# Four-layer graph network on one core: another order of the gate products in layer 0, another start and end of layer 3

## The chip, the cores and the metric

The kernel runs on one core of one Trainium2 chip, in one launch. The metric is device time in microseconds (us), the median of three runs; lower is better. A core has five engines that run side by side and are synchronised by semaphores: TensorE (matrix products and transposes, written PE in the profile; PEld is its loading of weights), VectorE (DVE), ScalarE (ACT), GpSimd (POOL) and SyncE (SP, which only issues transfers here). Matrix products land in PSUM banks[...]; everything else lives in the 128 partitions of SBUF.

## What is computed

The input x has 128 x 64 = 8192 tokens of 256 channels, all float32: 128 graphs of 64 nodes. Four layers of graph networks are applied in turn, each as

```
x = x + layer(relu(layernorm(x)))
```

Layer 0 is two graph convolutions, and then four LSTMs with windows of p = 1, 2, 3, 4 nodes, each of which writes the last state of every window back into the nodes:

```python
h = relu(einsum('ts,bsh->bth', adj, x @ Wg0 + bg0))
h = relu(einsum('ts,bsh->bth', adj, h @ Wg1 + bg1))
for p in range(1, 5):
    nw = Tv // p
    wins = h[:, :nw * p, :].reshape(Bv * nw, p, Hd)
    last = lstm_last(Wih[p-1], Whh[p-1], bih[p-1], bhh[p-1], wins)
    h = h.at[:, arange(nw) * p + (p - 1), :].set(last.reshape(Bv, nw, Hd))
# one step of the LSTM
g = x_t @ Wih.T + h @ Whh.T + bias          # gates i, f, gg, o of 256 channels each
c = sigmoid(f) * c + sigmoid(i) * tanh(gg)
h = sigmoid(o) * tanh(c)
```

Layer 1 is an attention over 512 edges with 4 heads. Layer 2 is a graph convolution, a product with W1, a batch norm with ReLU, a product with W2 and a second batch norm (over all tokens). Layer 3 is an attention over the 64 nodes of each graph:

```python
Wh = einsum('bnf,fo->bno', h, W)
e = leaky_relu((Wh @ a1)[:, :, None] + (Wh @ a2)[:, None, :], 0.2)
e = where(adj == 0, -inf, e)
out = einsum('bij,bjo->bio', softmax(e), Wh)
```

## The kernel before

The tokens are worked on in 16 chunks of 512 (`NCH`), or, in the LSTMs, in 4 groups of 2048 (`NGR`). A framework's scheduler puts the instructions of each engine into an order and sets the semaphores; an instruction that is wrapped in `late(...)` keeps its place in the order in which the program names it. So the order on an engine is in part written out and in part the scheduler's. Each engine then runs its own list strictly in order.

**The LSTMs of layer 0** take from 193 to 1281 us. The product of a gate (256 input channels by 256 output channels, both halved) is made with seven block products instead of eight, of inputs that are sums and differences of the halves (`xop` for the inputs, `lstm_h` for the state, computed in `prepare` and `gate_done`). The weights are combined in the same way by GpSimd and VectorE when a new window begins (line L434). A `Step` is one time step t of a window length w for one part of the tokens; its gates are i, gg, f, o, or only i, gg, o at t = 0, where there is no earlier state. A matmul of a product has 512 columns for w = 1, 256 for w = 2 and 4, and 336 for w = 3. For t = 0 a product is one matmul (with the input), for t > 0 two (input, state), all issued by L643. The trace shows each matmul as two passes.

The two halves of the groups are done one after the other, and in each half w = 1, 2, 3, 4. Within a window length the steps alternate between two parts of the tokens: t = 0 of one part, t = 0 of the other, t = 1 of the one, and so on. Such a pair of parts is what is called a pair below; w = 1 and 2 have two pairs per half, w = 3 and 4 one. There are 184 gates, 48 of them with t = 0 and w > 1.

`gate` is a generator that makes a gate's seven products, in four portions, with three accumulators in PSUM: `pa` (3 banks in turn), `pb` (2 banks) and `pc` (3 banks). The result goes to four blocks of the tile `gate`:

- products 1 (to `pa`) and 2 (to `pb`); then the copy of `pa` on ScalarE (L686), the addition of `pb` on VectorE (L687) and the gate's function, sigmoid or tanh, on ScalarE (L671)
- product 6, on top of 1 in `pa`; the copy of that sum on ScalarE (L691); product 7 to `pc` and the copy of it on ScalarE (L693)
- product 5, on top in `pa`; VectorE adds the sum to the copy of `pc` (L696)
- product 3, on top in `pa`, and the function straight from the bank (L671); product 4 on top in `pc`, VectorE adds it to the copy of L691 (L701), and the function of the two second blocks (L671). Then `gate_done` does the elementwise work of the cell.

Each of these products writes to a bank that the copy before it reads, so product 6 waits for L686, product 5 for L691, product 3 for L696, and product 4 for L693. A new gate waits until a bank of `pa` has been read by the last L671 of an older gate.

The slots of the loop (L805 and on) interleave three gates: in every slot a new one begins, the one before it (the middle) does its third portion, and the oldest ends:

```python
one = step.gate(new[1]); next(one)        # new gate: products 1, 2
if len(flight) > 1:
    next(flight[-1][1])                   # middle gate: product 5
    old = flight.pop(0)
    next(old[1], None)                    # oldest gate: products 3, 4
...
next(one)                                 # new gate: products 6, 7
```

`prepare` of the next step (copies by ScalarE, L624, differences by VectorE, L626 and after) is called near the end of the step before.

**The end of layer 2** leaves its output, before the last batch norm, in the first of the two tiles of each chunk's `hs`, and the batch norm as a scale and a shift per channel (`scale2`, `shift2`), which are known only when the last chunk's sums are in.

**Layer 3** takes from 1931 us to the end. For a chunk n, `fetch` loads the residual x; `second_norm` scales layer 2's output to the tile `o` (pool `xin2`, 4 buffers; chunk 0 on VectorE, L1598, and ScalarE, L1601, all others on GpSimd, L1606), transposes it into two banks (`pair`, L1613), adds the residual (L1615), takes mean and variance of each tile of 128 tokens (L1619, L1620), takes the inverse root by power on GpSimd (L1622 to L1626) and normalises (L1630 on GpSimd; chunk 0 L1634 on ScalarE). `features` transposes the result back (L1645) with ReLU on ScalarE (L1648); `project3` makes Wh, with one column more for the node's own score (two matmuls of 257 columns per tile, in halves of two tiles); `dense_scores` makes the scores and their exponentials; `turn` transposes these; `dense_values` makes the weighted sums (L50 into `pair`), divides and adds the residual (L1719) and stores 512 KB (L1727). The main loop runs the chunks in a pipeline: `second_norm(n + 2)`, `features(n + 1)`, `project3(n)`, `turn(n - 1)`, the rest of `project3(n)`, `dense_scores(n)`, `dense_values(n - 1)`, for n from -2 on. Transfers are issued on SyncE, but for the intermediate x of layer 0, which GpSimd issues.

Of the kernel before, what the change touches and what calls it, by code (L numbers as in the profile page):

```python
# [30 lines left out]
def gnn_stack_kernel(ctx: ExitStack, tc: tile.TileContext, a: dict, out: bass.AP):  # L31
# [25 lines left out]
    def token_tiles(ap, n=0):  # L57
        return ap[n * CHUNK : (n + 1) * CHUNK, :].rearrange("(i p) d -> p i d", p=P)
# [12 lines left out]
    def late(ins):  # L71

        tc.keep_in_program_order(ins)
# [334 lines left out]
    with ExitStack() as l0:  # L408
# [178 lines left out]
        class Step:  # L587
# [90 lines left out]
            def gate(self, q):  # L678
# [14 lines left out]
                nc.scalar.copy(blk[1, 1], pc[:, :N])  # L693
# [115 lines left out]
        for slot in range(len(tasks) + 2):  # L809
# [5 lines left out]
            if len(flight) > 1:  # L815
                next(flight[-1][1])
                old = flight.pop(0)
                next(old[1], None)
            elif flight and not new:
                old = flight.pop(0)  # L820
                next(old[1], None)
            else:
                old = None
                if flight:
                    next(flight[-1][1])
# [475 lines left out]
    with ExitStack() as l2:  # L1301
# [282 lines left out]
        def as_tokens(t):  # L1584
            return t.rearrange("p c t -> p (c t)").rearrange("p (i d) -> p i d", i=4)
# [4 lines left out]

        def second_norm(n):


            xt, v = xts[n], hs[n][0]
            half = (0, 1) if n % 2 == 0 else (1, 0)
            o = xin2.tile([P, 2, CHUNK], F32, tag="xin2", name="o")
            if n == 0:
                nc.vector.tensor_scalar(  # L1598
                    o[:, 0, :], v[:, half[0], :], scale2[:, 0:1], shift2[:, 0:1], ALU.mult, ALU.add
                )  # L1600
                nc.scalar.activation(  # L1601
                    o[:, 1, :], v[:, half[1], :], AF.Identity, bias=shift2[:, 1:2], scale=scale2[:, 1:2]
                )
            else:
                for c in range(2):
                    nc.gpsimd.tensor_scalar(  # L1606
                        o[:, c, :], v[:, half[c], :], scale2[:, c : c + 1], shift2[:, c : c + 1], ALU.mult, ALU.add
                    )
            p = pair_bank()
            for i in range(4):  # L1610
                for c in range(2):
                    k = (i % 2 * 2 + c) * P
                    nc.tensor.transpose(p[:, i // 2, k : k + P], o[:, c, i * P : (i + 1) * P], ident)  # L1613
            flat = xt.rearrange("p i d -> p (i d)")
            nc.vector.tensor_tensor(flat, p.rearrange("p b d -> p (b d)"), flat, ALU.add)  # L1615
            st = stat.tile([P, 4, 6], F32, tag="ln_st", name="ln_st")
            mv = stat.tile([P, 4, 2], F32, tag="ln_mv", name="ln_mv")
            for i in range(4):
                nc.vector.bn_stats(st[:, i, :], xt[:, i, :])  # L1619
                nc.vector.bn_aggr(mv[:, i, :], st[:, i, :])  # L1620
            rs = stat.tile([P, 4], F32, tag="ln_rs", name="ln_rs")
            nc.gpsimd.tensor_scalar(rs, mv[:, :, 1], 1e-5, None, ALU.add)  # L1622
            nc.gpsimd.tensor_tensor(rs, rs, half_power, ALU.pow)
            nm = stat.tile([P, 4], F32, tag="ln_nm", name="ln_nm")
            nc.gpsimd.tensor_tensor(nm, mv[:, :, 0], rs, ALU.mult)
            nc.gpsimd.tensor_scalar(nm, nm, -1.0, None, ALU.mult)  # L1626
            h = norms[n] = as_tokens(v)
            for i in range(4):
                if n:
                    nc.gpsimd.tensor_scalar(  # L1630
                        h[:, i, :], xt[:, i, :], rs[:, i : i + 1], nm[:, i : i + 1], ALU.mult, ALU.add
                    )
                else:
                    nc.scalar.activation(  # L1634
                        h[:, i, :], xt[:, i, :], AF.Identity, bias=nm[:, i : i + 1], scale=rs[:, i : i + 1]
                    )
# [75 lines left out]
        def dense_values(n):  # L1712
# [14 lines left out]
            nc.sync.dma_start(out=token_tiles(out, n), in_=xt)  # L1727
# [3 lines left out]
        for n in range(-2, NCH + 1):  # L1731
            if 4 <= n + 4 < NCH:
                fetch(n + 4)
            if n + 2 < NCH:
                second_norm(n + 2)
            if 0 <= n + 1 < NCH:
                features(n + 1)
# [77 lines left out]
```

## Time and profile before

| | us |
|---|---|
| median of 3 runs | 2097.78 |
| range of the runs | 2097.69 to 2099.34 |
| the profiled execution, whole | 2098.59 |
| its span in the trace | 2096.8 |

| stretch of the trace | from, to (us) | length | TensorE busy |
|---|---|---|---|
| layer 0, graph convolutions | 0 to 193 | 193.0 | 182.6 |
| layer 0, LSTMs | 193 to 1280.9 | 1087.9 | 1060.0 |
| layer 1 | 1280.9 to 1705 | 424.1 | 408.1 |
| layer 2 | 1705 to 1931 | 226.0 | 220.7 |
| layer 3 | 1931 to 2096.8 | 165.8 | 146.4 |

The span is what lies between the first and the last instruction of the trace, the profiled execution's own time is a little longer, and both stand for one execution among the runs. The mean clock that TensorE was granted is 0.988 of full speed over the span, and 0.93 in layer 3. Names such as `pa`, `pb`, `pc`, `bank` and `pair` in the profile are PSUM buffers, `gate`, `xop`, `lstm_h`, `o` and `h` tiles in SBUF. "L643" is line 643 of the kernel; a row `PE pa L643 <- ACT gate L691` is idle time of TensorE before a matmul of L643 into `pa` that ended with ScalarE's instruction of L691, with the total in us, the number of such waits and the longest.

### The profile page before, as it was taken

The numbers are of one execution on the slowest core, as the hardware profiler recorded it, in microseconds if no ns is written. First come the engines' busy times: TensorE is split into PE (matmuls) and PEld (weight loads), VectorE is DVE, ScalarE is ACT, GpSimd is POOL, SyncE is SP. The second block draws the span as 40 slices with busy tenths as digits, with TensorE's granted clock in tenths as the row PEclk, the third lists the DMA queues.
The fourth block names the chain that finished last, engine by engine and source line by source line (L and its number), as shares of the span: only waits on it lengthen the run. The fifth ranks groups of instructions, "written<-read, shape, count | busy, mean of one in ns | idle before, by whom it ended". The sixth has DMA issues, their size and how long they took to land.

```text
span 2096.8 us, 25494 instructions
## 1 busy us (share of the span) xinstructions
PE 2017.9 (96%) x9444; PEld 1356.4 (65%) x9444; DVE 1348.9 (64%) x2453; ACT 1186.4 (57%) x2264; POOL 321.3 (15%) x432
## 2 busy tenths in 40 slices
PE   8999999999999999999999998999999899999898
PEld 6776488866688746886667885333334775444686
DVE  8764666564655576556546555676766777886675
ACT  4344766554655468566546553666665456591454
POOL 3000010100200020002000002214323520001662
PEclk9999999999999999999999999999999999999899
DMA  9231000100100350001001006113224851022012
GB/s 314 93 96 51 0 21 1 41 0 1 40 1 1 105 177 21 1 1 41 0 0 41 1 1 226 61 51 96 81 76 120 254 191 51 1 80 81 31 61 71
DMA packets 94444, 135.06 MB, mean 64 GB/s; under 512 B 6384, under 2 KB 82032, under 8 KB 92144
## 3 DMA queue, kind: packets, MB, share of 16 engines
q1 hardware_dynamic: 87600, 109.11, 15.8%
q0 software_dynamic: 6112, 24.12, 3.8%
q8 instruction: 74, 1.21, 0.2%
q14 instruction: 50, 0.41, 0.1%
q10 hardware_dynamic: 608, 0.20, 0.0%
HBM read 87.28 MB, written 46.14 MB: 64 GB/s over the span
## 4 chain that ended last, share of the span: by engine, by line
PE 84%; ACT 5%; DVE 5%; issue 4%; DMA 1%; POOL 1%; ACTq 0%; POOLq 0%; DVEq 0%; SPq 0%
PE pa L643 25%; PE bank L50 12%; PE pc L643 12%; PE pb L643 6%; PE bank L947 5%; PE pa L1360 5%; PE pair L963 5%; PE bank L1141 3%; PE bank L979 2%; PE pc L1360 2%; ACT gate L671 2%; PE pair L50 1%; PE pb L1360 1%; ACT gate L723 1%; PE pair L1121 1%
## 5 line engine op out<-in xcount | busy, mean ns | idle before, releaser
L643 PE MATMUL pa<-xop,sih 128*128 128x256 f32 (+2 forms) x1056 | 347.4, 418 | 11.0 <-ACT gate L691 9.4
L671 ACT ACTIVATE gate<-gate,bias 128x256 f32<-128x256 f32 (+2 forms) x368 | 246.9, 678 | 181.2 <-DVE gate L687 97.5
L643 PEld LDWEIGHTS pa<-xop,sih 128*128 128x128 f32 x1056 | 199.3, 191 | 85.1 <-issue 20.9
L643 PE MATMUL pc<-xop,wih 128*128 128x256 f32 (+2 forms) x736 | 251.5, 423 | 0.0
L643 PE MATMUL pa<-lstm_h,shh 128*128 128x256 f32 (+1 forms) x672 | 212.6, 398 | 0.0
L687 DVE TENSOR_TENSOR gate<-pb,gate 128x256 f32<-128x256 f32 (+2 forms) x184 | 87.6, 476 | 162.2 <-PE pb L643 126.3
L970 DVE SCALAR_TENSOR_TENSOR lr<-lr 128x1024 f32<-128x1024 f32 x128 | 150.3, 1217 | 63.9 <-ACT lr L969 57.8
L643 PEld LDWEIGHTS pc<-xop,wih 128*128 128x128 f32 x736 | 140.1, 190 | 51.4 <-issue 22.5
L701 DVE TENSOR_TENSOR gate<-pc,gate 128x256 f32<-128x256 f32 (+2 forms) x184 | 87.7, 477 | 119.8 <-PE pc L643 118.3
L969 ACT COPY lr<-pair 128x1024 f32<-128x1024 f32 x128 | 123.0, 1013 | 49.8 <-PE pair L963 48.9
L643 PEld LDWEIGHTS pa<-lstm_h,shh 128*128 128x128 f32 x672 | 127.7, 190 | 30.2
L643 PE MATMUL pc<-lstm_h,whh 128*128 128x256 f32 (+1 forms) x448 | 141.8, 398 | 0.0
L686 ACT COPY gate<-pa 128x256 f32<-128x256 f32 (+2 forms) x184 | 76.8, 417 | 104.0 <-PE pa L643 103.4
L671 ACT ACTIVATE gate<-pa,bias 128x256 f32<-128x256 f32 (+2 forms) x184 | 94.6, 514 | 72.4 <-PE pa L643 71.4
L963 PE MATMUL pair<-sd_hot,xq 64*128 64x512 f32 x512 | 128.0, 619 | 2.3 <-ACT lr L969 2.3
L947 PE MATMUL bank<-wlv,hT 128*128 128x512 f32 x256 | 118.4, 605 | 0.2 <-ACT hT L156 0.2
L696 DVE TENSOR_TENSOR gate<-pa,gate 128x256 f32<-128x256 f32 (+2 forms) x184 | 87.5, 476 | 35.3 <-PE pa L643 33.1
L643 PE MATMUL pa<-xop,wih 128*128 128x256 f32 (+1 forms) x320 | 101.8, 400 | 5.6 <-ACT xop L624 3.1
L434 POOL TENSOR_TENSOR sih<-wih 128x512 f32<-128x512 f32 x8 | 10.4, 1306 | 630.5 <-DMA wih<-in_WihT 630.5
L643 PE MATMUL pb<-xop,wih 128*128 128x256 f32 (+1 forms) x320 | 100.9, 399 | 0.0
L643 PEld LDWEIGHTS pc<-lstm_h,whh 128*128 128x128 f32 x448 | 85.1, 190 | 20.1
L693 ACT COPY gate<-pc 128x256 f32<-128x256 f32 (+2 forms) x184 | 76.3, 415 | 32.5 <-PE pc L643 31.0
(321 smaller groups left out, 3820.9 us busy)
## 6 DMA issues: line engine op xcount, KB each, us to landing
field<-sd_hot SPq DMA_DIRECT2D x8, 1152.0 KB, 10.7
wih<-in_WihT SPq DMA_DIRECT2D x8, 1024.0 KB, 4.9
xres<-in_x SPq DMA_DIRECT2D x16, 512.0 KB, 5.9
xa<-xres POOLq DMA_DIRECT2D x16, 512.0 KB
xin<-xb SPq DMA_DIRECT2D x16, 512.0 KB, 3.9
h<-xb SPq DMA_DIRECT2D x16, 512.0 KB, 3.9
out_x<-h SPq DMA_DIRECT2D x16, 512.0 KB, 2.9
xin<-in_x SPq DMA_DIRECT2D x15, 512.0 KB, 7.5
```

The costliest lines, as they stand in the source:

```text
L50: nc.tensor.matmul(o, lhsT, rhs, start=start, stop=stop)
L643: ins = nc.tensor.matmul(p[:, : self.N], weights[kind, self.phase](k, q), x[k], start=first_ and kind == "ih", stop=kind == "hh" or not se ...
L671: nc.scalar.activation(out, in_, AF.Tanh if q == 2 else AF.Sigmoid, bias=bias[:, self.w - 1, 2 * q + j : 2 * q + j + 1],)
L686: nc.scalar.copy(blk[0, 0], pa[:, :N])
L687: nc.vector.tensor_tensor(blk[0, 0], pb[:, :N], blk[0, 0], ALU.add)
L696: nc.vector.tensor_tensor(blk[1, 1], pa[:, :N], blk[1, 1], ALU.add)
L701: nc.vector.tensor_tensor(blk[1, 0], pc[:, :N], blk[1, 0], ALU.add)
L947: ins = nc.tensor.matmul(p, hTs[n][:, k, i * P : (i + 1) * P], wlv[:, k, :], start=k == 0, stop=k == 1)
L963: ins = nc.tensor.matmul(p[:, par, :], queries[it][r, c * P : (c + 1) * P], sd_hot[r, :], start=True, stop=True)
L969: nc.scalar.copy(lr, p)
L970: nc.vector.scalar_tensor_tensor(lr, lr, 0.2, lr, ALU.mult, ALU.max)
L1360: ins = nc.tensor.matmul(p, lhs[k], x[k], start=first_, stop=last_one, skip_group_check=True)
```

## The change

It has four parts.

1. In each slot of the LSTM loop, the oldest gate's last portion (products 3, 4) is now asked for before the middle gate's product 5, so that a slot is: new 1, 2; oldest 3, 4; middle 5; new 6, 7.
2. The copy of product 7 from `pc` is done by VectorE for steps with t = 0 and w > 1, by ScalarE otherwise.
3. Layer 3 has a `first_norm` for chunk 0 alone. It works by pairs of tiles (256 tokens): half-width scalings on VectorE and ScalarE, four transposes into one bank, addition, mean and variance, the root by ScalarE's Sqrt and VectorE's reciprocal, the normalisation on ScalarE, and then transposes back and ReLU by pair. The scaling of the other chunks is a function of its own, `scale_o`, still on GpSimd, and is called two chunks ahead of `second_norm`, for chunks 1 to 3 ahead of everything else. Chunk 1 takes its root like chunk 0, and has two of its four tiles normalised by ScalarE and two by GpSimd. For chunks 1 and 2 some instructions keep their place (`late`), and for chunk 0 the first projection (tiles 0, 1) comes before `second_norm(2)`, the second after it.
4. The last chunk's result is stored in two halves, each after its two tiles, instead of in one.

```diff
@@ gate
-                nc.scalar.copy(blk[1, 1], pc[:, :N])
+                (nc.vector.tensor_copy if not self.t and self.w > 1 else nc.scalar.copy)(blk[1, 1], pc[:, :N])
@@ the slot loop
             if len(flight) > 1:
-                next(flight[-1][1])
                 old = flight.pop(0)
                 next(old[1], None)
+                next(flight[-1][1])
@@ layer 3
+        def first_norm():
...
+            for ip in range(2):
+                r = slice(ip * 256, (ip + 1) * 256)
+                late(nc.vector.tensor_scalar(
+                    o[:, 0, r], v[:, 0, r], scale2[:, 0:1], shift2[:, 0:1], ALU.mult, ALU.add
+                ))
+                late(nc.scalar.activation(
+                    o[:, 1, r], v[:, 1, r], AF.Identity, bias=shift2[:, 1:2], scale=scale2[:, 1:2]
+                ))
+            def add(ip):
+                p = bank()
...
+                        ins = nc.tensor.transpose(
+                            p[:, (2 * i + c) * P : (2 * i + c + 1) * P], o[:, c, k : k + P], ident
+                        )
...
+                late(nc.vector.tensor_tensor(flat, p, flat, ALU.add))
+            def sums(ip):
+                i2 = slice(2 * ip, 2 * ip + 2)
+                for i in (2 * ip, 2 * ip + 1):
+                    late(nc.vector.bn_stats(st[:, i, :], xt[:, i, :]))
+                    late(nc.vector.bn_aggr(mv[:, i, :], st[:, i, :]))
+                late(nc.scalar.activation(rs[:, i2], mv[:, i2, 1], AF.Sqrt, bias=eps))
+            def root(ip):
+                i2 = slice(2 * ip, 2 * ip + 2)
+                late(nc.vector.reciprocal(rs[:, i2], rs[:, i2]))
+                late(nc.vector.scalar_tensor_tensor(
+                    nm[:, i2], mv[:, i2, 0], -1.0, rs[:, i2], ALU.mult, ALU.mult
+                ))
+                for i in (2 * ip, 2 * ip + 1):
+                    late(nc.scalar.activation(
+                        h[:, i, :], xt[:, i, :], AF.Identity, bias=nm[:, i : i + 1], scale=rs[:, i : i + 1]
+                    ))
+            add(0)
+            sums(0)
+            add(1)
+            root(0)
+            sums(1)
+            root(1)
+            yield
...
+            for ip in range(2):
+                p = bank()
...
+                late(nc.scalar.activation(
+                    hT[:, :, ip * 256 : (ip + 1) * 256].rearrange("p c (i t) -> p i c t", i=2),
...
+                    AF.Relu,
+                ))
+                yield
+        def scale_o(n):
...
+            for c in range(2 if n else 0):
+                late(nc.gpsimd.tensor_scalar(
+                    o[:, c, :], v[:, half[c], :], scale2[:, c : c + 1], shift2[:, c : c + 1], ALU.mult, ALU.add
+                ))
         def second_norm(n):
...
+            keep = late if n < 3 else lambda ins: ins
...
+            yield
...
+            if n == 1:
+                keep(nc.scalar.activation(rs, mv[:, :, 1], AF.Sqrt, bias=eps))
+                keep(nc.vector.reciprocal(rs, rs))
+                keep(nc.vector.scalar_tensor_tensor(nm, mv[:, :, 0], -1.0, rs, ALU.mult, ALU.mult))
+            else:
...
-                if n:
+                if n > 1 or i > 1:
...
@@ dense_values
+                if n == NCH - 1 and i % 2:
+                    nc.sync.dma_start(
+                        out=token_tiles(out, n)[:, i - 1 : i + 1, :], in_=xt[:, i - 1 : i + 1, :]
+                    )
-            nc.sync.dma_start(out=token_tiles(out, n), in_=xt)
+            if n < NCH - 1:
+                nc.sync.dma_start(out=token_tiles(out, n), in_=xt)
@@ the loop of layer 3
+        for n in range(3):
+            scale_o(n)
+        start = first_norm()
+        next(start)
+        second = second_norm(1)
+        next(second)
+        for _ in start:
+            pass
+        project3(0, (0, 1))
+        for _ in second:
+            pass
+        scale_o(3)
-        for n in range(-2, NCH + 1):
+        for n in range(NCH + 1):
             if 4 <= n + 4 < NCH:
                 fetch(n + 4)
             if n + 2 < NCH:
-                second_norm(n + 2)
-            if 0 <= n + 1 < NCH:
+                for _ in second_norm(n + 2):
+                    pass
+            if n + 4 < NCH:
+                scale_o(n + 4)
+            if n == 0:
+                project3(0, (2, 3))
+                dense_scores(0)
+                features(1)
+                continue
+            if n + 1 < NCH:
                 features(n + 1)
```

In the built program the order of TensorE in LSTM slots is new 1, 2; oldest 3, 4; middle 5; new 6, 7, where the scheduler leaves it so; its order in layer 3 from chunk 2's projection to the end is the same as before. At layer 3's start TensorE's order was o(0), o(1), h(0), o(2), h(1) and then chunk 0's projection; it is now o(0), o(1), h(0), half of chunk 0's projection, o(2), the other half, chunk 0's scores, h(1) and on, where o(n) and h(n) are the eight transposes of chunk n's scaled output and of its normalised tokens.

## The prediction

> **What bounds the kernel now.** First the page's busy shares, then TensorE's waits by releaser, then the same waits in order of time, then the stretches around them.
>
> ```profile
> PE 2017.9 (96%) x9444; PEld 1356.4 (65%) x9444; DVE 1348.9 (64%) x2453; ACT 1186.4 (57%) x2264; POOL 321.3 (15%) x432
> ```
>
> TensorE is the bound: 2096.8 - 2017.9 = 78.9 us is all that it is not busy in. A change that adds or removes no product can gain only from that idle time and from a low clock. TensorE's own waits (total us, times, longest):
>
> ```profile
> PE pa L643 <- ACT gate L691: 9.4, 12, 1.5
> PE pair L1645 <- ACT h L1634: 6.0, 1, 6.0
> ...
> PE pair L1613 <- DVE o L1598: 4.0, 1, 4.0
> ...
> PE pa L643 <- ACT xop L624: 3.1, 2, 1.6
> ...
> PE pa L643 <- ACT gate L671: 2.3, 3, 1.1
> ...
> PE pa L643 <- ACT gate L686: 1.4, 4, 0.4
> ```
>
> The four rows with `pa` are the recurrent part of layer 0: 9.4 + 3.1 + 2.3 + 1.4 = 16.2 us. In order of time all of them lie in the pairs of t = 0 steps with w > 1, where a product is only 2 x 0.217 = 0.43 us (100 us from 300 hold 457 matmuls in 99.0 us busy). Both halves together: entering w = 2, 1.34 + 0.62 + 1.34 + 1.49 = 4.8; second pair of w = 2, 2 x (0.35 + 0.62) = 1.9; entering w = 3, 1.5 + 1.6 = 3.1; entering w = 4, 3.6 + 2.7 = 6.3. One of them, from the timeline:
>
> ```profile
> 269.54 1.54 ACT L671 ACTIVATE gate<-gate,bias 128x256 f32<-128x256 f32 x2
> ...
> 270.97 0.36 ACT L691 COPY gate<-pa 128x256 f32<-128x256 f32 x1
> ...
> 271.38 1.13 PE L643 MATMUL pa<-xop,sih 128*128 128x256 f32 x4 [1.34 <-ACT gate L691]
> ```
>
> The fifth product of the middle gate waits for the copy of its bank (L691), which stands on ScalarE behind two activations. VectorE is as full when w = 4 begins:
>
> ```profile
> 560.64 2.04 DVE L736 TENSOR_TENSOR hT<-gate 128x1344 f32<-128x1344 f32 x1 [1.52 <-ACT gate L671]
> 562.52 0.44 DVE L687 TENSOR_TENSOR gate<-pb,gate 128x256 f32<-128x256 f32 x1
> 562.85 1.85 DVE L626 TENSOR_TENSOR xop<-hT 128x512 f32<-128x512 f32 x1
> 564.62 0.41 DVE L696 TENSOR_TENSOR gate<-pa,gate 128x256 f32<-128x256 f32 x1
> 564.96 1.16 DVE L632 TENSOR_TENSOR xop<-xop 128x256 f32<-128x256 f32 x1
> ```
>
> The start of layer 3, by stretches (PE, PEld, DVE, ACT, POOL busy with counts, then the granted clock):
>
> ```profile
> 1935.00:1939.10 4.10, 3.90 (x16) 3.24 (x16) 1.23 (x1) 0.25 (x1) 4.10 (x6) 0.50 0.00 0
> 1939.10:1945.09 5.99, 0.03 (x1) 0.00 (x0) 4.45 (x17) 0.65 (x2) 5.49 (x11) 0.50 0.00 0
> 1945.09:1950.46 5.37, 5.37 (x24) 4.77 (x25) 1.43 (x2) 2.51 (x5) 4.74 (x9) 0.50 0.00 0
> 1950.46:1958.87 8.41, 8.41 (x49) 6.60 (x48) 5.00 (x15) 4.09 (x10) 5.91 (x11) 0.99 0.00 0
> ```
>
> TensorE idles 6 us while VectorE and then GpSimd normalise chunk 0, and runs at half clock until 1950.7: eight transposes take 1.9 us there and 1.04 us at 1956. From 1963.8 to 2060 it is busy in all of 96.2 us, so nothing is to be had in the steady part. The end:
>
> ```profile
> 2090.88 1.66 DVE L1719 SCALAR_TENSOR_TENSOR h<-pair,den,h 128x256 f32<-128x256 f32 x4 [4.22 <-PE pair L50]
> 2092.56 0.37 SPq L1727 DMA_DIRECT2D out_x<-h  x1
> ```
>
> [...] half clock from 1933.6 to 1950.7 is 17.1 us[...]. [...] 1283 ns for a table load, as the trace has for L1693; the new Sqrt activations stand before that load, behind a Sqrt (L1331) already there, and the built program has no load more.
>
> **The change part by part.** *Fifth product after the oldest gate's last.* Per slot TensorE did new 1, 2; middle 5; oldest 3, 4; new 6, 7; now new 1, 2; oldest 3, 4; middle 5; new 6, 7. No product is added. Between a gate's 6 and its 5 stand five products instead of three, so each L691 wait may shrink by two products: 0.87 us at 256 columns. A bank `pa` is free one product earlier, which helps the L671 waits. The price: between a gate's 5 and its 3 now stand four products instead of seven (1.7 us for 3.0), and 3 needs VectorE's add (L696). That is an added wait; all of TensorE is queued behind it.
>
> *Copy of `pc` to VectorE for t = 0, w > 1.* 48 of the 184 copies (L693) leave ScalarE (0.37 us each, about 0.27 from start to start in a full queue) for VectorE, about 0.34 from start to start. With queue spacings VectorE has per t = 0 gate 3 x 0.34 + (2 x 1.14 + 2 x 0.6 + 4 x 0.34)/3 = 2.6 us, and 2.95 with the copy, against 3.04 of TensorE; ScalarE falls from about 2.8 to 2.55. Neither is over the bound, but VectorE has hardly any slack left.
>
> I laid the new queue order over these durations, place by place. Entering w = 2: the third products wait 0.37, 0.25 and 0.4 us for the add and once 0.25 for L686; TensorE gains about 1.0 of 1.96 (first half), 1.5 of 2.83 (second). Second pair of w = 2: all L691 waits go, 0.15 is left, gain 0.8 twice. Entering w = 3: the add stands behind L626 (2.15 us there, while GpSimd sums weights), a new wait of about 0.8; gain 0.5 twice. Entering w = 4: the add of the second gate now stands behind L626 (1.85) and L632 (1.16), and its third product comes two matmul groups after the new gate's first; a new wait of some 2.3 us takes the place of the 1.38 + 0.26 + 0.37, and the `xop` wait stays: gain 0. Sum 1.0 + 1.5 + 1.6 + 1.0 = 5.1, less 0.5 for small waits at w = 1: **-4.6**. From both sides: all L691 and L671 waits go, -11; a 2.3 us wait in all eight pairs, 18.4 against 16.2 saved, +3 with w = 1. At the end of layer 0 the second last gate's sum comes 0.87 us sooner, but the last gate's 5, add and 3 stand bare: -0.3 (between +0.7 and -0.9).
>
> *Layer 3, chunk 0 by tile pairs.* On the clock of the profile before: scale ready 1934.4; half-width scalings end 1934.8 (VectorE) and 1934.95 (ScalarE, 0.52 as L1634); four transposes at 0.24 end 1936.1; add of 512 columns 0.69; two sums at 0.53 (the first norm of the kernel has four from 4.03 to 6.24) to 1937.9; square root, reciprocal, product 0.3 + 0.2 + 0.2 behind the second add, 1938.9; two activations to 1940.0; the second pair to 1941.8. Transposes, ReLU, first projection at 1942.4 in place of 1950.46. But work has been moved behind it: o(2) and h(1) came before it until now. At half clock eight matmuls of 257 columns (0.235 each at full clock) take 3.8 us, to 1946.2; with the clock back at about 1947, o(2) ends 1947.6 instead of 1949.0. Chunk 2's sums then wait in VectorE's order behind the add of chunk 0's scores, 1950.8; GpSimd's four small steps (1.95) and scaling (2.2) end 1956.6, no sooner than before. So h(2) ends near 1956.8; from there 4.75 us of products to the end of chunk 1's scores, 1961.6 in place of 1963.8, since the wait for the exponentials (1.5) is gone: **-2.7**, with a chance in four that the clock rises during the first transposes (then -5). Ends: -5.5[...].
>
> *Outputs scaled two chunks ahead, and chunk 1's norm halved between ScalarE and GpSimd.* 1.56 us of scaling per chunk stays on GpSimd, which waits 2.8 us per chunk for the sums (39.2 us in 14 waits): cover enough; without it, at most 1.56 per chunk. The steady order on TensorE is the same. SP's queue only gets one store more: zero.
>
> *Last store in halves.* The store's transfer ran from 2093.45 to 2095.05, 1.55 us; half of it starts 0.8 us sooner: **-0.75** (0 to -0.9).
>
> Sum: -4.6 - 0.3 - 2.7 - 0.75 = -8.35. The profiled execution took 2098.59 (span 2096.8 and 1.8 around it), 0.8 above the median; it would take 2090.2, the median 2089.4.
>
> **The rivals.** (a) VectorE takes over in layer 0: each L691 wait returns as a wait of the third product. For it: VectorE at 2.95 of 3.04 us. Against: the second pair of w = 2 has VectorE idle 0.7 to 1.0 us at a time. Then -3.75: 2094.0. (b) All L691 and L671 waits go and the clock rises early: -11 - 5 - 0.75 = -16.8, 2081.0. For it: the added slack, 0.87 us, is more than 8 of the 12 waits. Against: full VectorE at w = 3 and 4. (c) Slower: the third product waits for the add in every gate, not only at t = 0. At 184 gates it undoes the gain from 0.045 us a gate on, and is slower by 0.2% from 0.068; at 0.1 us it is +18.4 - 8.35 = +10, 2107.8. For it: four products in place of seven everywhere. Against: with t > 0 or w = 1 four products are 3.4 us, and the add that the trace shows late (222.53, after a product that ended 220.8) is 2.4 us behind at its end.
>
> **How the numbers follow.** Forecast 0.60, (a) 0.15, (b) 0.15, (c) 0.10. The forecast's own range is 2085 to 2094. The range 2081.5 to 2097 leaves out half of (b) and nearly all of (c). What this measurement can tell from no change is 0.2%, 4.2 us. Faster by more: 0.9 of the forecast, almost half of (a), all of (b): 0.76; slower: 0.8 of (c), 0.08; the rest, 0.16, is the same.
>
> **What would show it.** Right: waits for L691 below 2.5 us, a new wait of TensorE for VectorE's add behind the fifth product of 3 to 5 us at w = 3 and 4; `xop` near 3; first projection of layer 3 some 7.5 us after its first transpose (15.4 before), but chunk 1's scores only about 2 us sooner; the last transfer half as long. Wrong: waits for that add at w = 1 or t > 0 (then c), none at w = 4 (then b), or transposes at 0.13 us before 1940 on this clock.

## The result, and the profile after

The changed kernel takes 2090.43 us (median of 6 runs, 2088.75 to 2093.68); the kernel before, run beside it, 2098.56 us (6 runs, 2097.11 to 2101.14). The ratio is 0.9965, with a 95% interval from 0.9955 to 0.9975: 7.3 us less, between 5 and 9. The forecast was 2089.4 us, within 2081.5 to 2097.0. In a later series the same kernel gave 2089.98 us (5 runs), ratio 0.9966 (0.9952 to 0.9979).

The profiled execution took 2088.75 us, its span is 2086.8, 10.0 less than before. The table cuts the span at marks that both traces have: the first product of the LSTMs, the last one, the first transpose of the residual after it, the last product of layer 2, the first projection of layer 3, the end of chunk 1's scores, and the start of the last weighted sums. The last column is a second profiled execution of the changed kernel.

| stretch (us) | before | after | difference | after, again |
|---|---|---|---|---|
| start to first LSTM product | 192.48 | 192.98 | +0.50 | 192.74 |
| first to last LSTM product | 1082.88 | 1077.72 | -5.16 | 1078.98 |
| from there to the first transpose of layer 0's result | 5.52 | 4.26 | -1.26 | 4.27 |
| from there to layer 2's last product | 650.19 | 650.63 | +0.44 | 648.91 |
| to layer 3's first projection | 19.39 | 11.32 | -8.07 | 10.98 |
| from there to the end of chunk 1's scores | 13.32 | 18.92 | +5.60 | 19.81 |
| from there to the last weighted sums | 123.32 | 123.78 | +0.46 | 123.42 |
| last weighted sums to the end | 9.71 | 7.20 | -2.51 | 8.71 |

First the page's busy shares and then TensorE's waits (total us, times, longest) of the changed kernel:

```profile
PE 2016.4 (97%) x9444; PEld 1353.1 (65%) x9444; DVE 1362.5 (65%) x2509; ACT 1180.1 (57%) x2222; POOL 317.7 (15%) x422
```

```profile
PE pa L643 <- DVE gate L697: 7.7, 9, 1.6
...
PE bank L1616 <- DVE o L1605: 3.8, 1, 3.8
...
PE pa L643 <- ACT gate L686: 3.2, 4, 1.2
...
PE pa L643 <- ACT xop L624: 2.6, 2, 1.3
...
PE pair L1730 <- POOL h L1715: 1.8, 1, 1.8
```

The 9.4 us of waits for L691 and the 2.3 for L671 are gone. In their place stand waits for VectorE's add behind product 5, now L697: the row named in advance. The waits in the LSTMs' products fell only from 16.2 to 7.7 + 3.2 + 2.6 + 0.4 = 13.9 us, less than the time gained. A wait is counted from the modelled end of the matmul before it, and with 256 columns that end lies 0.38 us after the start, while the next matmul starts after 0.216 us where nothing holds it back: every wait in the list is shorter than the delay. Counted from start to start, the delays within the LSTMs' products fell from 26.0 to 20.6 us.

The timeline where w = 4 begins in the first half shows what the third product waits for:

```profile
560.63 1.28 POOL L434 TENSOR_TENSOR sih<-wih 128x512 f32<-128x512 f32 x1 [139.67 <-DMA wih<-in_WihT]
560.76 2.14 DVE L626 TENSOR_TENSOR xop<-hT 128x512 f32<-128x512 f32 x1
...
562.78 0.45 DVE L702 TENSOR_TENSOR gate<-pc,gate 128x256 f32<-128x256 f32 x1
563.11 1.20 DVE L632 TENSOR_TENSOR xop<-xop 128x256 f32<-128x256 f32 x1
...
564.24 0.41 DVE L697 TENSOR_TENSOR gate<-pa,gate 128x256 f32<-128x256 f32 x1
...
564.70 0.48 PE L643 MATMUL pa<-xop,sih 128*128 128x256 f32 x1 [1.40 <-DVE gate L697]
```

The add itself is short (0.41 us). It stands behind L626 and L632, which take 2.14 and 1.20 us here while GpSimd sums weights; in the second half, where GpSimd begins later, the same two take less, and there is no such wait in this trace (0.79 us in the second one):

```profile
1105.46 1.04 DVE L626 TENSOR_TENSOR xop<-hT 128x512 f32<-128x512 f32 x1
...
1106.98 0.42 DVE L632 TENSOR_TENSOR xop<-xop 128x256 f32<-128x256 f32 x1
```

The start of layer 3, TensorE alone:

```profile
1929.42 1.97 PE L1616 MATMUL bank<-ident,o 128*128 128x128 f32 x8 [3.83 <-DVE o L1605]
...
1936.91 3.79 PE L50 MATMUL bank<-wext,hT 128*128 128x257 f32 x8
1940.49 1.78 PE L1689 MATMUL pair<-ident,o 128*128 128x128 f32 x8
...
1949.28 2.06 PE L1730 MATMUL pair<-ident,h 128*128 128x128 f32 x8 [1.84 <-POOL h L1715]
```

The first projection begins 7.5 us after the first transpose, but chunk 2's transposes of o and the rest of chunk 0's projection now come behind it, and TensorE then waits 1.84 us for GpSimd's scaling of chunk 2. Of 8.07 us 2.47 are left. At the end the last weighted sums ran mostly at half clock before (3.68 us, with a granted clock of 0.54, the first line) and at full clock after (2.00 us, with 1.00, the second):

```profile
2087.10 3.68 PE L50 MATMUL pair<-wh,field 128*128 128x256 f32 x8 [0.90 <-ACT field L1708]
...
2079.61 2.00 PE L50 MATMUL pair<-wh,field 128*128 128x256 f32 x8 [0.91 <-ACT field L1793]
```

### The profile page after: what moved, and what is told of

It is laid out like the page before. It is cut to its first block, busy times and chain, and to the rows that moved or that the text cites. A ratio compares the mean times of both kernels' runs of the same rounds, so it can differ in the third digit from the quotient of the medians.

```text
span 2086.8 us, 25504 instructions
## 1 busy us (share of the span) xinstructions
PE 2016.4 (97%) x9444; PEld 1353.1 (65%) x9444; DVE 1362.5 (65%) x2509; ACT 1180.1 (57%) x2222; POOL 317.7 (15%) x422
## 4 chain that ended last, share of the span: by engine, by line
PE 85%; DVE 7%; ACT 3%; DMA 2%; issue 1%; POOL 1%; SPq 0%; ACTq 0%; POOLq 0%; DVEq 0%
PE pa L643 25%; PE pc L643 13%; PE bank L50 12%; PE pb L643 6%; PE pa L1361 5%; PE pair L964 5%; PE bank L948 5%; PE bank L1142 3%; PE bank L980 2%; PE pc L1361 2%; PE pb L1361 1%; PE pair L50 1%; ACT gate L671 1%; PE pair L1122 1%; PE bank L167 1%
## 5 line engine op out<-in xcount | busy, mean ns | idle before, releaser
L671 ACT ACTIVATE gate<-gate,bias 128x256 f32<-128x256 f32 (+2 forms) x368 | 247.4, 679 | 172.4 <-DVE gate L687 89.1
L702 DVE TENSOR_TENSOR gate<-pc,gate 128x256 f32<-128x256 f32 (+2 forms) x184 | 87.6, 476 | 119.5 <-PE pc L643 119.2
L686 ACT COPY gate<-pa 128x256 f32<-128x256 f32 (+2 forms) x184 | 76.0, 413 | 96.2 <-PE pa L643 95.8
L697 DVE TENSOR_TENSOR gate<-pa,gate 128x256 f32<-128x256 f32 (+2 forms) x184 | 87.3, 475 | 44.0 <-PE pa L643 43.4
L691 ACT COPY gate<-pa 128x256 f32<-128x256 f32 (+2 forms) x184 | 75.5, 410 | 59.0 <-PE pa L643 57.6
L671 ACT ACTIVATE gate<-pa,bias 128x256 f32<-128x256 f32 (+2 forms) x184 | 93.9, 510 | 25.9 <-PE pa L643 24.3
L434 POOL TENSOR_TENSOR sih<-wih 128x512 f32<-128x512 f32 x8 | 10.6, 1325 | 626.1 <-DMA wih<-in_WihT 438.9
```

The costliest lines, as they stand in the source:

```text
L671: nc.scalar.activation(out, in_, AF.Tanh if q == 2 else AF.Sigmoid, bias=bias[:, self.w - 1, 2 * q + j : 2 * q + j + 1],)
L686: nc.scalar.copy(blk[0, 0], pa[:, :N])
L697: nc.vector.tensor_tensor(blk[1, 1], pa[:, :N], blk[1, 1], ALU.add)
L702: nc.vector.tensor_tensor(blk[1, 0], pc[:, :N], blk[1, 0], ALU.add)
```

## The experiments

The time from the first LSTM product to the first transpose after the last is called "LSTMs" below: 1088.4 us before, 1082.0 after. Layer 1, with the same code in all, took from 418.9 to 424.0 us in the traces, from its first transpose to layer 2's first product, so that single stages are compared as well as whole runs. The LSTMs scatter too: the same code took 1088.4 and 1087.1 us (before and start_only) and 1082.0, 1083.2 and 1083.4 (the changed kernel twice and chunk2_split), so that a difference of 1.3 us between two traces tells nothing, and the gain lies between 3.7 and 6.4 us. Each ratio is to the kernel before in the same series.

| run | median (us) | ratio to before, 95% | LSTMs (us) | first LSTM product |
|---|---|---|---|---|
| changed kernel | 2090.43 | 0.9965 (0.9955 to 0.9975) | 1082.0 | 193.0 |
| slot_only | 2093.31 | 0.9968 (0.9955 to 0.9980) | 1081.5 | 193.1 |
| copy_only | 2100.69 | 1.0008 (0.9999 to 1.0016) | 1087.2 | 192.7 |
| start_only | 2095.21 | 0.9987 (0.9981 to 0.9994) | 1087.1 | 192.8 |
| no_copy | 2088.74 | 0.9950 (0.9936 to 0.9963) | 1081.7 | 193.2 |
| five_last | 2103.81 | 1.0024 (1.0015 to 1.0033) | 1096.1 | 192.5 |
| chunk2_split | 2089.60 | 0.9958 (0.9944 to 0.9972) | 1083.4 | 192.7 |
| no_sums | 2077.73 | 0.9893 (0.9878 to 0.9908) | 1071.4 | 192.6 |
| sums_in_dram | 2087.71 | 0.9946 (0.9932 to 0.9960) | 1069.9 | 199.4 |
| sums_early | 2088.94 | 0.9960 (0.9947 to 0.9974) | 1071.6 | 203.2 |
| sums_early_no_copy | 2088.50 | 0.9954 (0.9941 to 0.9968) | 1071.6 | 201.6 |
| changed_again | 2089.98 | 0.9966 (0.9952 to 0.9979) | 1083.2 | 192.7 |
| sums_gated | 2079.32 | 0.9908 (0.9891 to 0.9924) | 1072.8 | 192.6 |

**The order of the slot alone (slot_only).** The kernel before, with

```diff
             if len(flight) > 1:
-                next(flight[-1][1])
                 old = flight.pop(0)
                 next(old[1], None)
+                next(flight[-1][1])
```

> The kernel before with the order of the slot alone (oldest gate's 3, 4 ahead of the middle gate's 5); the copy of product 7 stays on ScalarE, layer 3 is that of before. Measured from the first LSTM product to the first transpose at the start of layer 1, the LSTMs take 1088.4 us before and 1082.0 after the whole change. Theory A (the two products of slack between 6 and 5 do it): 1083.5 or less, so at least 5 of the 6.4 us, waits for L691 below 3 us in all, the whole run 0.9975 of before. Rival B (it is the ScalarE queue, a copy shorter, that does it): the slack alone leaves more than half of the 9.4 us of L691 waits, 1086 or more, the whole run 0.999.

The LSTMs took 1081.5 us, as little as with the whole change, so that the order alone has all of the gain there. Its waits in the LSTMs:

```profile
PE pa L643 <- DVE gate L696: 5.9, 10, 1.5
...
PE pa L643 <- ACT xop L624: 1.9, 2, 1.0
PE pb L643 <- DVE gate L687: 1.9, 1, 1.9
PE pb L643 <- ACT xop L624: 1.2, 2, 0.6
PE pa L643 <- ACT gate L691: 0.2, 1, 0.2
```

Of the L691 waits 0.2 us are left. The drain after the last product is 4.26 us here too. Theory A holds; rival B falls.

**The copy alone (copy_only).**

```diff
-                nc.scalar.copy(blk[1, 1], pc[:, :N])
+                (nc.vector.tensor_copy if not self.t and self.w > 1 else nc.scalar.copy)(blk[1, 1], pc[:, :N])
```

> The kernel before with the copy of product 7 on VectorE for t = 0 and w > 1 alone. Theory A: ScalarE's queue is a copy of 0.37 us shorter, the L691 waits stay above 6 of 9.4 us, the LSTMs take 1087 to 1088.5 us (1088.4 before), the whole run within 0.1% of before. Rival B: the L691 waits fall below 4 us and the LSTMs take 1085 or less, the whole run 0.998. Rival C (VectorE becomes the bound): new waits of TensorE for VectorE, the LSTMs over 1089.

```profile
PE pa L643 <- ACT gate L691: 9.0, 13, 1.4
...
PE pa L643 <- ACT xop L624: 3.6, 2, 1.8
```

The L691 waits stay at 9.0 us, the LSTMs are within theory A's range (1087.2), and the time can't be told from that of before. The same from the other side: **the changed kernel without the copy (no_copy)**, the diff above undone.

> The changed kernel with the copy of product 7 back on ScalarE everywhere; order of the slot, layer 3 and last store as changed. Theory A (the copy on VectorE is worth nothing beside the new order, since VectorE's queue is what the third product waits for): the LSTMs take 1081 to 1082 us as with the order alone (1081.5), waits for the add (L697) near 5.9 us instead of 7.7, the whole run 2087 to 2090.5, not slower than the changed kernel; the parts measured alone give 0.9968 x 0.9987 = 0.9955. Rival B (the copy carries a part of the gain in the changed kernel): the waits for L691 come back (over 3 us), the LSTMs 1084 or more, the whole run 2092 or more.

LSTMs 1081.7 us, waits for the add 6.0 us, and no wait for L691 in the list. The run is not slower than the changed kernel; whether it is faster can't be told, as the two intervals overlap.

**The start of layer 3 alone (start_only).** The kernel before with the third part of the change, of which this is the order of the work:

```diff
+        for n in range(3):
+            scale_o(n)
+        start = first_norm()
+        next(start)
+        second = second_norm(1)
+        next(second)
+        for _ in start:
+            pass
+        project3(0, (0, 1))
...
```

> The LSTMs of before with the new start of layer 3 alone (chunk 0 by tile pairs, outputs scaled two chunks ahead, chunk 1 halved); the last store is in one piece. Theory A: from the last product of layer 2 to the first projection of layer 3 it is 8 us less than the 19.4 of before, but from there to the end of chunk 1's scores most of it is lost again (the second half of chunk 0's projection and chunk 1's transposes now come after, and TensorE waits some 1.8 us for GpSimd's normalisation of chunk 2), so 2.5 us are left; the whole run 2 to 3 us below before, ratio 0.9988. Rival B: the steady part takes the rest back too (chunk 1's gain is gone by the last chunk), ratio 1.000. [...]

The first projection came 11.31 us after layer 2's last product (19.39 before), chunk 1's scores ended 30.17 us after it (32.71), so 2.5 us were left; from there to the last weighted sums 123.78 us (123.32). Ratio 0.9987. Theory A holds. With the store in one piece the last weighted sums begin 8.03 us before the end, at the same full clock as in the changed kernel (eight matmuls in 2.00 us in both), where it is 7.20 us: the halved store is worth 0.8 us.

**Product 5 at the end of the slot (five_last).** The changed kernel, with the middle gate's 5 after the new gate's 6 and 7:

```diff
             if len(flight) > 1:
                 old = flight.pop(0)
                 next(old[1], None)
-                next(flight[-1][1])
+                if not new:
+                    next(flight[-1][1])
...
             if new:
                 next(one)
+                if old:
+                    next(flight[-1][1])
```

> The changed kernel with the middle gate's product 5 after the new gate's 6 and 7, as the last of the slot: two products in place of four between a gate's 5 and its 3, seven in place of five between its 6 and its 5. Theory A (the distance to the add is the price of the order, and it was nearly used up): waits for the add (L697) grow from 7.7 to over 20 us, at t > 0 too, where two products are 1.7 to 2.3 us and VectorE's cell work of 1.5 to 3 us may stand ahead of the add; the run is 10 to 30 us slower than the changed kernel. Rival B (VectorE's add is early enough everywhere but beside GpSimd's sums): waits for it stay under 12 us, the run within 4 us of the changed kernel.

```profile
PE pa L643 <- DVE gate L697: 14.2, 19, 1.7
```

The run lost all that the change had gained, 14.1 us in the LSTMs, within theory A's range; rival B's 4 us are far off. The listed waits grew less than theory A had it, to 14.2 us, and stand nearly all where t is 0. Counted from start to start, the delays within the products grew by 13.4 us, and 7.1 us of that are delays of 30 to 150 ns, below what the wait list shows: 120 of them in place of 40, half of the growth at t > 0, where the changed kernel has next to none. So, of the three places tried, the one between is the best: with three products between 6 and 5 TensorE waits for ScalarE, with two between 5 and 3 for VectorE. (Between 6 and 5 there are eight products in this run, not the seven of the expectation.)

**Chunk 2's normalisation split (chunk2_split).**

```diff
-                if n > 1 or i > 1:
+                if n > 2 or i > 1:
```

> The changed kernel with chunk 2's normalisation also split, two tiles on ScalarE and two on GpSimd. Theory A (the start of layer 3 is bound by GpSimd's scaling of chunk 2, 2.2 us in one row): TensorE's wait of 1.8 us for it becomes 0.8 or less, the scores of chunk 1 end 29.2 us or less after layer 2's last product (30.2 now), the whole run 1 us below the changed kernel. Rival B: ScalarE is at chunk 0's exponentials just then, the wait stays or moves to ScalarE, no gain or up to 1 us slower.

```profile
PE pair L1730 <- ACT h L1719: 1.4, 1, 1.4
...
PE bank L50 <- ACT wh L1754: 0.7, 1, 0.7
```

The wait moved to ScalarE, 1.4 us, and one of 0.7 for ScalarE's copy of a projection came up that is not in the changed kernel's list; chunk 1's scores ended at 30.21 us as before. Rival B holds.

**Without the sums of the weights (no_sums).** The changed kernel, from the fourth set of weights on without the loop of L434, so that it leaves out work that the LSTMs need:

```diff
+                made.append(kind)
+                if len(made) > 3:
+                    self.of = {1: a11, 2: a12, 3: a12, 4: a22, 5: a21, 6: a11, 7: a21}
+                    return
                 for o, x, y, op in (
```

> The changed kernel without GpSimd's sums of the weights (L434) from the second window length on; the products take the loaded blocks themselves, so that the sums and differences of weights are left out. Theory A (the waits that are left at w = 3 and w = 4 come from VectorE running at half speed beside GpSimd's sums): L626 takes about 1.1 us in place of 2.1 wherever it stood beside the sums, TensorE's waits for the add (L697) fall from 7.7 to under 3.5 us, the LSTMs take 1077 to 1079.5 us (1082.0 after the change), the whole run 2 to 5 us below the changed kernel. Rival B (VectorE's queue is too full by itself): the waits for L697 stay above 6 us, the LSTMs within 1 us of 1082.0.

All that is left of TensorE's waits in the LSTMs' products (their line is L649 here, L630 is the copy to `xop`, L692 that of product 1, L703 the add):

```profile
PE pa L649 <- ACT xop L630: 2.7, 2, 1.3
PE pa L649 <- ACT gate L692: 1.5, 2, 0.8
PE pa L649 <- DVE gate L703: 1.2, 3, 0.6
```

The direction is theory A's, the size is more than twice what it had: the LSTMs lost 10.6 us and not 2.5 to 5. What the sums do to VectorE shows in the durations (min/median/max in ns) of the first difference for `xop`, first in the changed kernel, then without the sums:

```profile
L626 DVE TENSOR_TENSOR xop<-hT x44: 674/1098/2175, 254.6 to 1221.3; 128x512 f32<-128x512 f32 x32, 128x672 f32<-128x672 f32 x12
```

```profile
L632 DVE TENSOR_TENSOR xop<-hT x44: 679/1095/1151, 254.2 to 1210.4; 128x512 f32<-128x512 f32 x32, 128x672 f32<-128x672 f32 x12
```

In the changed kernel's trace at w = 4, GpSimd's sums begin at 560.63 (1.28 us), 561.99 (2.05) and 563.99 (1.45). L626 and L632, with both inputs in SBUF, begin beside the first and the second and take 2.14 and 1.20 us; in the same place of no_sums they take 1.07 and 0.43. L702 and L697, with one input in PSUM, begin beside the second and the third and keep their 0.45 and 0.41 us; in no_sums they take 0.43 and 0.42. Why the one pair grows and the other does not is not shown.

**The sums made once (sums_in_dram, sums_early, sums_early_no_copy, sums_gated).** If the sums cost that much where they stand, they may be made during the graph convolutions, stored in DRAM, and loaded with the weights: nothing is left out. In all of these runs, but for the names of the buffers:

```diff
-                    out=t.rearrange("p k q j m -> p k (q j m)"), in_=a[f"W{kind}T"][:, w - 1]
+                    out=flat, in_=a[f"W{kind}T"][:, w - 1] if kept is None else kept[0]
...
+                if kept is not None:
+                    nc.sync.dma_start(out=s, in_=kept[1])
+                    return
...
+                nc.gpsimd.dma_start(out=kept[0], in_=flat)
+                nc.gpsimd.dma_start(out=kept[1], in_=s)
```

The run sums_in_dram makes them from the seventh chunk of the convolutions on.

> The changed kernel with the sums of the weights made once, during the graph convolutions, stored in DRAM, and loaded with the weights (1.75 MB in place of 1 MB) whenever a window length begins; nothing is left out. Theory A (GpSimd's sums at the windows' beginnings are what slows VectorE there): the LSTMs take 1070 to 1074 us, as without the sums (1071.4; changed kernel 1082.0), the first LSTM product comes no later than 194 us (193.0), the whole run 2076 to 2082. Rival B (the sums cost what they cost wherever they are, or the loads come late): the convolutions grow by 5 us or more, or TensorE waits for a transfer at the first step t = 1 of a window, the whole run over 2085.

LSTMs 1069.9 us, as theory A had it, but the first LSTM product came at 199.4 us, as rival B had it. The convolutions by stretches of 20 us (PE, PEld, DVE, ACT, POOL, then the clock):

```profile
80.00:100.00 20.00, 20.00 (x111) 15.46 (x110) 19.86 (x33) 6.85 (x13) 9.66 (x10) 1.00 0.84 305
100.00:120.00 20.00, 14.19 (x62) 11.08 (x61) 19.96 (x42) 5.97 (x12) 11.58 (x13) 0.83 0.79 311
```

VectorE is full beside the sums, and TensorE loses 5.8 us. The next run makes the sums in a buffer of their own, which the program fills from the thirteenth chunk on, with the loads on GpSimd's queue:

```diff
+                if n == 12:
+                    for kind in ("hh", "ih"):
+                        for w in (3, 4):
+                            Weights(kind, w, ahead).keep()
+                    for one in (weights["ih", 0], weights["ih", 1], weights["hh", 1]):
+                        one.keep()
```

> As the run with the sums in DRAM, nothing left out, but the sums for w = 3 and 4 are made in a buffer of their own from the thirteenth chunk of the graph convolutions on, where VectorE is half idle (8.65 to 12.5 of 20 us from 120 us on), loaded and stored on GpSimd's queue; those for w = 1 and 2 stay where the changed kernel has them. Theory A (it was VectorE, full from 80 to 120 us beside the sums, that made the convolutions 6.4 us longer): first LSTM product by 194 us, LSTMs 1069 to 1072 us, the whole run 2076 to 2081, 0.991 of before or less. Rival B (making and storing the sums costs the same elsewhere): first LSTM product after 197 us or LSTMs over 1074, the whole run 2084 or more.

> The same with the copy of product 7 on ScalarE everywhere. Theory A (VectorE is no longer late, so the copy's place hardly matters): LSTMs within 1.5 us of the kernel with the copy on VectorE. Rival B (with VectorE relieved the copy on VectorE is worth its place): LSTMs 2 us or more longer, waits for L691 back.

In both the convolutions grew, to 203.2 and 201.6 us to the first LSTM product: the scheduler had put the loads near the head of GpSimd's queue, where nothing held them back, and in the first of the two runs the first load went out at 4.68 us, into the stretch in which the transfers are busiest (in the changed kernel 310 GB/s over the first 52 us, against a mean of 65):

```profile
4.68 0.79 POOL L432 DMA_DIRECT2D wahead<-in_WhhT  x1
14.41 1.26 POOL L447 TENSOR_TENSOR sahead<-wahead 128x512 f32<-128x512 f32 x1 [8.93 <-DMA wahead<-in_WhhT]
```

In the LSTMs the place of the copy makes no difference here either (1071.6 in both). The last run ties the loads to the work, issues them on SyncE, and has the copy of product 7 on ScalarE:

```diff
+                    late(nc.gpsimd.tensor_copy(flat[:, 0, :1], hTs0[1][:, 1, 0, UNIT - 1 : UNIT]))
+                    nc.sync.dma_start(out=flat, in_=a[f"W{kind}T"][:, w - 1])
```

> The sums for w = 3 and 4 again made once and kept in DRAM, with the copy of product 7 on ScalarE; this time GpSimd first copies one number of chunk 7's result into the buffer, so that the loads can't start before that chunk is done, at some 110 us (in the run before they ran from 5 us on, since nothing held them back, and the first LSTM product came at 201.6). Nothing is left out. Theory A: the convolutions are as long as in the changed kernel, first LSTM product by 195 us, LSTMs 1071.6 within 1 us, the whole run 2077 to 2082, below 0.992 of before. Rival B: four loads, sums and stores one after another don't fit into the 80 us that are left, the first LSTM product comes after 199 us, the whole run 2085 or more.

```profile
111.85 0.18 POOL L432 COPY wahead<-hT 128x1 f32<-128x1 f32 x1 [79.00 <-ACT hT L575]
117.22 1.27 POOL L448 TENSOR_TENSOR sahead<-wahead 128x512 f32<-128x512 f32 x1 [5.19 <-DMA wahead<-in_WhhT]
...
171.18 1.26 POOL L448 TENSOR_TENSOR wahead<-wahead 128x512 f32<-128x512 f32 x1
```

The sums now lie between 117 and 172 us, where TensorE stays busy throughout (92.6 us of the 92.6 from 100 us on); the first LSTM product comes at 192.6 us. The LSTMs take 1072.8 us. At 2079.32 us, ratio 0.9908 (0.9891 to 0.9924), it beats both kernels; the kernel to set beside it, with the copy in the same place, is no_copy at 0.9950.

**The changed kernel once more (changed_again).**

> The changed kernel itself once more. If layer 1, whose code is the same in all of these kernels and which took from 418.3 to 423.4 us in their traces, scatters by transfers alone, it will again lie anywhere in that range; LSTMs 1082.0 within 1 us, chunk 1's scores 30.2 us after layer 2's last product. The last weighted sums took 2.0 us (full clock) with the new start of layer 3 in five of six traces and 3.6 us in all of the others[...].

LSTMs 1083.2 us, a little outside the 1.0 expected; layer 1 took 418.9 us by the marks above, the shortest of all, and chunk 1's scores ended 30.79 us after layer 2's last product. The clock ran differently at the start of layer 3: it rose for one stretch of 3.4 us at 1932.7, and fell again. The last weighted sums took 3.49 us, near the 3.68 at a granted clock of 0.54 and far from the 2.00 at full clock above, so that they ran mostly at half clock with the new code as well.

## Why the prediction was right, step by step

- **LSTM products, -4.6: -5.16, in the second trace -3.90, and -3.6 as the mean over all traces of the same LSTM code** (two of before, three of after). The mechanism is the one given: the slack between 6 and 5 takes the L691 waits away, and a part comes back as waits for the add. By window length, from the first product of one to the first of the next, both halves together and as means: w = 2 gained 3.8 (4.1 forecast); w = 3 lost 0.4 where 1.0 was to be gained; w = 4 gained 0.15 where 0 was put, with a scatter of more than 1 us in its second half, so that the 0.5 and 1.45 of the first pair of traces tell nothing; w = 1 stayed the same within 0.1, where 0.5 was to be lost. The term that was mis-sized is w = 3: the waits for the add were put at 0.8 us in each half and are about 2.0 and 2.2. They come from GpSimd's sums, for in no_sums w = 3 has none of these waits and takes 149.2 us in each half in place of 151.8 and 152.0. At w = 4 a wait of 2.3 us was forecast; it is 1.40 in the first half and 0 or 0.79 in the second, where L626 beside no sum takes 1.04 us and not the 1.85 that both halves were given; and 1.16 us for L686 in each half was not foreseen. That the sum came out so near is in part luck, since these misses go both ways.
- **The copy** was part of that sum with no price of its own; copy_only and no_copy show no gain from it: with the new order the LSTMs took 1081.5 and 1081.7 us without it, 1082.0 to 1083.4 with it. The fear that it would leave VectorE without slack (rival a) was unfounded: in no_sums, with the copy on VectorE, the waits for the add are 1.2 us, so that what makes VectorE late is GpSimd.
- **The end of layer 0, -0.3: about -0.7.** The step had a gain and a price, and both came. The gain is the row of -1.26 above, for 0.87 forecast: the second last gate's work on the state is done earlier, and what ends last is now the last gate's own function. The price is the last gate's third product, which waits for the add with nothing to fill the time; that wait, 0.59 us at 1268.71, lies before the last product and so in the row of the products. Together this is -0.67, within the bounds given. With products and end taken together, the LSTMs gained 4.9 us by the means over the traces, as forecast.
- **Start of layer 3, -2.7: -2.47.** The first projection gained 8.07 us (8.06 forecast); the loss of most of it to the moved work and to GpSimd's chunk 2 came as given. The two times in that step differ by 2.2 us, and 2.7 went into the sum. The clock rose at 1942.0 us, which is 1947.5 on the clock of the profile before, for about 1947 forecast, and the transposes of h(2) ended at 1951.3, which is 1956.8 there, as forecast: chunk 2 sets the pace.
- **Last store, -0.75: -0.8** (8.03 to 7.20). The two times given for the store's transfer are 1.60 us apart, not 1.55; and the L691 and L671 waits of the bounds add up to 11.7 us, not 11. Neither changes the forecast.
- **Not in the sum:** the last weighted sums ran at full clock in this execution, -1.7 us, and in other stretches together +1.4 was lost. The +1.4 is small beside layer 1, which scatters by 5 us with the same code. The clock of the last sums goes with the new start of layer 3 in most traces, full in 9 of 11 with it and in none of the 3 without; but changed_again and sums_in_dram have the new start and half clock, and no run shows why, so it stays open whether this belongs to the change. By the first pair of traces the parts of the forecast give -9.7 where -8.35 was forecast, with the means for the LSTMs -8.2, and the runs 7.3.
- **Rival (c)** needed a wait in every gate. At the change's distance there is one wait for the add at t > 0, 0.59 us at the very end, and none at w = 1. Five_last shows that it was near: two products closer and the gain is gone.
- **Rival (b)** was right that the L691 and L671 waits would all go, but the new waits came. Its early clock did not: the first eight transposes of layer 3 took 1.97 us, at half clock (0.50 granted), and the clock rose at the forecast's time. What further gain was to be had in the LSTMs lay in the sums, as no_sums shows.

## What to carry to other kernels

When a wait for an engine's copy sits behind other work in that engine's queue, moving the consumer two products back can pay more than moving the copy to another engine; how far back is a balance with the next wait in the chain, to be priced on both sides, and by window length or stage, since a sum can come out right by misses that cancel. An engine that is busy for a seventh of the time, as GpSimd is here, may still be the one that sets the waits, through the instructions of its neighbour that it doubles (here L626, from 1.04 to 2.14 us): look at the longest durations of a row, not at its median. Work that is moved to a quiet stretch must be tied to it by a dependency; in sums_early its place in the program did not hold it back (sums_gated changed the queue of the loads as well).

## What was not expected of the hardware

- The sums on GpSimd within the LSTMs, 44 of 1.27 us each when alone, cost the LSTMs about 10 us, through VectorE's subtractions going from 1.04 to 2.14 and from 0.42 to 1.20 us beside them.
- A load of 1 MB issued by GpSimd took 9.9 us to arrive at 53.5 us (9.7 us for the one at 4.7), one issued by SyncE 5.2 to 7.6 us between 112 and 167 us; the traffic around them differed, so the share of the queue in this is open.
- TensorE was busy for 5.84 of 7.51 us at the start of layer 3 (78%), and its granted clock stayed at 0.50 all that time. In the changed kernel's trace the clock was at 0.50 from 1928.34 to 1942.00 us, with TensorE busy for 7.51 us of the first 10.24 and for all of the last 3.42, and at 1.00 from then to 2085.36. In the trace before it was at 0.50 from 1933.63 to 1950.70, with TensorE busy for 9.54 of 17.07 us. What it takes for the clock to rise is not shown.
